# Four-layer graph network: one sign flipped in layer 0, one transpose of layer 3 moved to memory, the last graph's layer 3 in two halves

## The chip, the cores and the metric

One Trainium2 chip, one core of it. The metric is device time in microseconds (us): the median over the executions of one program. The engines are PE (matrix multiply; PEld is its weight load), DVE (vector), ACT (scalar, with the activation functions), POOL (GpSimd) and SP, which here only issues DMAs.

## The reference

64 graphs of 256 nodes with 128 features share one adjacency matrix `adj` (256 x 256). Four layers follow each other, each `x = x + layer(relu(layernorm(x)))`.

```
# layer 0, h = relu(layernorm(x)), e runs over 256 channels; W is adj
s1 = h @ W[:, :128].T ;  s2 = h @ W[:, 128:].T
pre[i,j,e] = s1[i,e] + s2[j,e] + b_lin[e]
e[i,j] = sum_e a[e] * leaky_relu(pre[i,j,e], 0.2) + adj[i,j]
out = sigmoid(softmax_j(e) @ h)
# layer 1: attention of one sigmoid per pair, masked by adj, two linear maps with elu
# layer 2: A = exp(8*tanh(q k'/sqrt(128)/8)) * adj, rows normalised;  out = A @ x @ v
# layer 3: five steps of a gated unit, av = [adj @ h, adj @ h]
z = sigmoid(av @ w3' + u3(h)); r = sigmoid(av @ w4' + u3(h))
hv = tanh(av @ w5' + (r*h) @ u5'); h = (1-z)*h + z*hv
```

Layer 0 is by far the most work: for each graph 256 x 256 x 256 values of `relu(s1 + s2 + b)`, each used once in a sum over channels. All is float32.

## The kernel before, in words

**Groups.** The graphs are taken in 34 groups: two of one graph, thirty of two graphs, two of one graph (`GROUPS`). Names below follow the profile: lines are those of the kernel before.

**Layer 0.** `head` (L558) makes, for a group, `s1` and its negative `s1n`, with channels on the partitions: two ACT instructions for each half of the channels, L576 and L578, both from the same PSUM tile. `senders` (L608) makes `s2` for one graph. The relu is written as a maximum: `relu(s1+s2) = max(s2, -s1) + s1`, and the `+ s1` is the same for all j and falls out of the softmax. So three engines make tiles of 128 channels x 256 senders, one per receiving node: ACT with `Relu(s2 + s1)` (L758), POOL with `max(min(s2, FLT_MAX), s1n)` (L763), DVE with `max(s2, s1n)` (L740), four or eight nodes in one instruction. PE multiplies the tiles by the weights `a` and sums over channels (`multiply`, L824). The weights stand in `a_win`, a column of +-0.8 in a field of zeros, of which a window of 32 columns is loaded so that node t falls in row t of the output. A batch is eight tiles (4 blocks of 32 rows x 2); where both tiles of a block have the same weight column, one matmul of 512 columns does them (four matmuls a batch), else two of 256 (eight a batch).

PE and the makers share work through merging: when enough batches wait for PE (`SPARE`), `begin` (L666) lays out the next two rows so that DVE adds the second channel half to the first (`merge`, L782) and PE gets three batches in place of four.

**Layers 1 to 3** run as chains of small pieces beside layer 0 of later graphs. Many transposes go through memory: `crossed` (L106) writes a tile to DRAM and reads it back with its two axes exchanged, both DMAs in SP's queue; the read is in pieces of 16 bytes for a group of two graphs. In layer 3 the groups 0 to 27 do so (`layer3_across`, L1206: state in after the norm, and after each of the first four steps); the state of the last step is transposed by PE into PSUM (`y_ps`, L151) and DVE adds it to x (L1269). Groups 28 to 33 (`layer3`) transpose by PE at every step (`hn_ps`). PSUM for layer 3 is one pool that the two lanes take in turn (the list `inside`).

**Order.** All engine instructions are written out by a planner (the loop from L1411 on). It keeps a clock for each engine, advanced by fixed costs per instruction, asks every chain when its next piece could start, and emits the piece or tile that starts first; at equal times the order of the list `chains` decides. A DMA read carries a planned landing time, and what uses it is not planned earlier. A change of cost anywhere therefore moves the order of tiles everywhere.

**The end.** When the last tile is made, layers 1 to 3 of the last graph (group 33) and layer 3 of groups 31 and 32 are left; they share PE. Group 33's layer 3 is 256 columns wide and uses the banks of `ps_e` and `ps_h` (`Home.LAST`).

Of the kernel before, what the change touches and what calls it, by code (L numbers as in the profile page):

```python
# [12 lines left out]
P = 128  # L13
# [61 lines left out]
def kernel(ctx: ExitStack, tc: tile.TileContext, ins: dict, out: bass.AP):  # L75
# [124 lines left out]
    a_win = constant([P, 2, 63], "a_win")  # L200
# [53 lines left out]
    blin_n = constant([P, 2], "blin_n")  # L254
# [3 lines left out]
    def constants0():  # L258
# [59 lines left out]
        dve(2).tensor_scalar(blin_n, b_ps, -1.0, None, ALU.mult)  # L318
        for half in (1, 0):
            yield "act"  # L320
            act(N).copy(w_p[:, half, :], p[:, half, :])
# [18 lines left out]
        for c in range(2):  # L340
            w = a_win[:, c, 31:32]
            dve(1).tensor_scalar(w, p_two[:, c : c + 1], n_pos, None, ALU.is_lt)
            dve(1).tensor_scalar(w, w, 1.6, -0.8, ALU.mult, ALU.add)

# [182 lines left out]
    def first_head(xt, to, snd):  # L527
# [14 lines left out]
        s1n = ap.tile([P, 2, W], F32, tag="s1n", name="s1n")  # L542
        for ec in range(2):
            dve(W, 1).tensor_scalar(
                s1n[:, ec, :], s1_ps[:, ec, :], -1.0, blin_n[:, ec : ec + 1], ALU.mult, ALU.add
            )
# [3 lines left out]
        s1 = ap.tile([P, 2, W], F32, tag="s1", name="s1")  # L550
        for ec in range(2):
            act(W, 1, more=27).activation(
                s1[:, ec, :], s1_ps[:, ec, :], AF.Identity, bias=blin_p[:, ec : ec + 1]
            )
        to.update(s1=s1, s1n=s1n)
        snd.update(s2=s2, s2_ps=s2_ps)

    def head(xt, to):  # L558
# [7 lines left out]
        for ec in range(2):  # L566
# [6 lines left out]
            if ec == 0:  # L573
                s1 = ap.tile([P, 2, W], F32, tag="s1", name="s1")
                s1n = ap.tile([P, 2, W], F32, tag="s1n", name="s1n")
            act(W, 1, more=27).activation(s1[:, ec, :], p, AF.Identity, bias=blin_p[:, ec : ec + 1])  # L576
            yield "act"
            act(W, 1, more=27).activation(  # L578
                s1n[:, ec, :], p, AF.Identity, bias=blin_n[:, ec : ec + 1], scale=-1.0
            )  # L580
        to.update(s1=s1, s1n=s1n)
# [53 lines left out]
    class Pairs:  # L635
# [5 lines left out]
        def __init__(self, g, b, of, snd):  # L641
# [9 lines left out]
            self.s1n_v = of["s1n"].rearrange("p c (g t k) -> p c g k t", g=4, k=G)[  # L651
# [14 lines left out]
        def begin(self):  # L666
# [7 lines left out]
            for t, ec, on_top, two in kinds:  # L674
                batch = {
                    "t": t, "ec": ec, "merged": on_top, "two": two, "halves": 0, "ready": 0.0
# [42 lines left out]
        def make(self, who):  # L719
# [9 lines left out]
            s1, s1n = self.of["s1"], self.of["s1n"]  # L729
            if who == "dve":  # L730
# [4 lines left out]
                if batch["two"]:  # L735
                    s1n = self.s1n_v[:, ec, 2 * g2 : 2 * g2 + n, 1, t : t + 2].unsqueeze(3)
                else:
                    s1n = self.s1n_v[:, ec, 2 * g2 : 2 * g2 + n, :, t : t + 1]
# [4 lines left out]
                    s1n.to_broadcast([P, n, 2, N]),  # L743
                    ALU.max,
# [7 lines left out]
            else:  # L752
                for g, ic, i in self.nodes(batch, g2):
                    if g > 2 * g2 or ic:
                        yield
                    if who == "act":
                        model.op("act", model.TILE["act"] + 42 * (s2 is self.snd["s2"]))
                        nc.scalar.activation(  # L758
                            r[:, g, ic, :], s2[:, ec, :], AF.Relu, bias=s1[:, ec, i : i + 1]
                        )  # L760
                    else:
                        model.op("pool", model.TILE["pool"])
                        nc.gpsimd.tensor_scalar(  # L763
                            r[:, g, ic, :], s2[:, ec, :], FLT_MAX, s1n[:, ec, i : i + 1],
# [7 lines left out]
        def merge(self):  # L772

            _, batch, g2 = self.merges.pop(0)
            r = batch["r"]
            for g, ic, i in self.nodes(batch, g2):
                if ic:
                    continue
                if g > 2 * g2:
# [3 lines left out]
                    r[:, g, ic, :], self.own("dve")[:, 1, :], self.of["s1n"][:, 1, i : i + 1],  # L783
                    r[:, g, ic, :], ALU.max, ALU.add,
# [18 lines left out]
        def multiply(self):  # L803
# [11 lines left out]
            elif batch["ec"]:  # L815
                parts = ((0, t, 0, 0), (1, t, 1, 1))
            else:
                parts = ((slice(0, 2), t, 0, slice(0, 2)),)
            for ic, t, sign, k in parts:
                for g in range(4):  # L820
                    to, of = self.e_ps[bass.ts(g, 32), ic, :], r[:, g, k, :]
                    if len(parts) == 1:
                        to, of = to.rearrange("p a b -> p (a b)"), flat(of)
                    nc.tensor.matmul(  # L824
                        to, lhsT=a_win[:, sign, 31 - t : 63 - t], rhs=of,
# [101 lines left out]
    def layer1(x1, h, h_t, at, last):  # L927
# [33 lines left out]
        yield "pool"  # L961
# [62 lines left out]
    def layer2(x2, by_memory):  # L1024
        G, NB, W = sizes(x2)
        h = yield from ln_relu(bp, x2, "h2", "h")
# [4 lines left out]
        else:  # L1031
            h_t = yield from by_pe(h, "h_t", when=free_a)
            yield "pe"
        g_ps = psum_a([P, W], "g_ps")
# [5 lines left out]
        hv_ps = psum_a([P, G, P], "hv_ps")  # L1040
# [7 lines left out]
        for b in range(NB):  # L1048
            yield "pe"
            s_ps = psum_a([P, 2, N], "s2_ps")  # L1050
# [477 lines left out]
```

## Time and profile before

| what | value |
|---|---|
| median of 3 runs | 4942.22 us (4939.57 to 4942.91) |
| the profiled execution's own time | 4945.24 us |
| its span | 4943.5 us |
| PE busy | 4882.2 us (99%) |
| DVE busy | 4855.4 us (98%) |
| ACT busy | 4824.6 us (98%) |
| POOL busy | 4773.1 us (97%) |
| DMA queue of SP, share of 16 engines | 73.8% |
| mean granted clock of PE | 1.0 |

Busy time of a group is the union of its instructions' intervals, and "mean ns of one" is the length of one from its start to its end. The engines overlap the end of one instruction with the start of the next, so what an instruction costs its engine is the distance from its start to the start of the one behind it, read from the timeline; it is shorter than the mean. A matmul in float32 shows as two records, so that four matmuls are eight.

### The profile page before, as it was taken

To read this page: it belongs to the slowest core of one execution; us is meant where nothing else is said; L and a number is where in the kernel's file an instruction comes from. 1 tells how busy PE (TensorE), PEld (TensorE's weight loads), DVE (VectorE), ACT (ScalarE), POOL (GpSimd) and SP (SyncE) were. 2 spreads that over 40 slices of the span, in tenths; PEclk is the share of its full clock that TensorE was granted. 3 is DMA by queue.
4 is the path that set the end of the run, shared out by engine and by line. 5 is a ranking of instruction groups with operands and counts; after the bars stand their busy time and mean duration, and the time that the engine had idled before them with its cause. 6 is when DMAs were issued, how large, how long until landed. Compare 5 with 4: busy or idle time off the path is not lost.

```text
span 4943.5 us, 176182 instructions
## 1 busy us (share of the span) xinstructions
PE 4882.2 (99%) x69407; PEld 2392.8 (48%) x69407; DVE 4855.4 (98%) x8488; ACT 4824.6 (98%) x12590; POOL 4773.1 (97%) x10419
## 2 busy tenths in 40 slices
PE   9999999999999999999999999999999999999998
PEld 4445544444554454545544544445444544445444
DVE  9999999999999999999999999999999999999994
ACT  8999999999999999999999999999999999999994
POOL 8999999999999999999999999999999999999891
PEclk9999999999999999999999999999999999999999
DMA  1559989989799889898898797787776777773220
GB/s 24 21 17 32 33 35 39 39 33 40 35 35 39 40 32 43 34 36 39 34 40 36 36 39 37 32 44 36 34 40 35 38 37 37 36 37 22 17 15 6
DMA packets 4456815, 165.39 MB, mean 33 GB/s; under 512 B 4386992, under 2 KB 4423728, under 8 KB 4455984
## 3 DMA queue, kind: packets, MB, share of 16 engines
q1 hardware_dynamic: 4455440, 153.86, 73.8%
q8 instruction: 544, 8.91, 1.0%
q14 instruction: 287, 2.35, 0.3%
q10 hardware_dynamic: 544, 0.26, 0.0%
HBM read 77.73 MB, written 76.35 MB: 31 GB/s over the span
## 4 chain that ended last, share of the span: by engine, by line
PE 50%; DVE 36%; ACT 5%; issue 2%; POOL 1%; DMA 0%; DVEq 0%; SPq 0%; ACTq 0%; POOLq 0%
PE e_ps L824 31%; DVE r L740 15%; DVE r L782 14%; PE gate_ps L144 4%; ACT r L758 3%; PE hv_ps L144 3%; PE m_ps L144 3%; PE s_ps L144 2%; PE o_ps L144 1%; PE e_ps L144 1%; PE rc_ps L144 1%; DVE bst L479 1%; PE rsum_ps L144 1%; DVE gate_ps L1255 1%; DVE rh L1253 1%
## 5 line engine op out<-in xcount | busy, mean ns | idle before, releaser
L763 POOL TENSOR_SCALAR r<-s,s1n 128x256 f32<-128x256 f32 x10168 | 4600.2, 478 | 40.5 <-PE e_ps L824 24.5
L758 ACT ACTIVATE r<-s_act,s 128x256 f32<-128x256 f32 x9736 | 4041.1, 758 | 5.4 <-PE e_ps L824 5.4
L824 PE MATMUL e_ps<-r,a_win 128*32 128x256 f32 (+1 forms) x40960 | 3293.8, 464 | 10.2 <-DVE r L740 7.9
L740 DVE TENSOR_TENSOR r<-s_ps,s1n 128x2048 f32<-128x2048 f32 (+1 forms) x1313 | 2341.5, 1818 | 0.3 <-PE e_ps L824 0.3
L824 PEld LDWEIGHTS e_ps<-r,a_win 128*32 128x32 f32 x40960 | 1404.0, 110 | 1609.1 <-issue 884.7
L782 DVE SCALAR_TENSOR_TENSOR r<-s_ps,s1n,r 128x256 f32<-128x256 f32 x4096 | 1687.0, 469 | 0.2
L501 ACT ACTIVATE h<-xt,bsh,brs 128x128 f32<-128x128 f32 x512 | 302.1, 791 | 19.7 <-DVE bsh L491 19.2
L758 ACT ACTIVATE r<-s,s 128x256 f32<-128x256 f32 x512 | 271.6, 775 | 0.0
L144 PE MATMUL m_ps<-adj_q,hn 128*32 128x256 f32 x4096 | 248.3, 379 | 2.1 <-ACT hn L1193 2.1
L144 PEld LDWEIGHTS m_ps<-adj_q,hn 128*32 128x32 f32 x4096 | 162.1, 132 | 93.9 <-issue 32.8
L488 POOL TENSOR_TENSOR brs<-bve,neg_half 128x4 f32<-128x4 f32 (+1 forms) x136 | 134.0, 985 | 66.0 <-DVE bve L484 60.8
L144 PE MATMUL gate_ps<-m_t,w_t 128*32 128x512 f32 (+1 forms) x1360 | 170.0, 567 | 1.5 <-ACT m_ps L1153 1.4
L144 PE MATMUL gate_ps<-m_t,t_w_w 128*32 128x512 f32 (+1 forms) x1360 | 170.5, 568 | 0.3 <-ACT m_t L1143 0.2
L144 PE MATMUL hv_ps<-m_t,t_w_w 128*32 128x512 f32 (+1 forms) x1360 | 170.1, 567 | 0.0
L144 PE MATMUL hv_ps<-rh,u_th 128*32 128x512 f32 (+1 forms) x1360 | 169.7, 567 | 0.0
L144 PE MATMUL s_ps<-h_t,w_p 128*32 128x256 f32 (+1 forms) x1568 | 138.7, 452 | 3.8 <-DVE adj_l L618 3.2
L144 PE MATMUL gate_ps<-hf,u_t 128*32 128x512 f32 (+1 forms) x1088 | 136.9, 567 | 0.0
L1232 ACT COPY m_t<-m_ps 128x512 f32<-128x512 f32 (+1 forms) x140 | 130.8, 934 | 1.2 <-PE m_ps L144 1.2
L1250 ACT ACTIVATE hv_ps<-hv_ps,bh 128x512 f32<-128x512 f32 (+1 forms) x140 | 128.7, 919 | 0.0
L1248 ACT ACTIVATE gate_ps<-gate_ps,bz 128x512 f32<-128x512 f32 (+1 forms) x140 | 127.5, 911 | 0.0
L1236 ACT ACTIVATE m_ps<-gate_ps,br 128x512 f32<-128x512 f32 (+1 forms) x140 | 116.4, 831 | 7.1 <-PE gate_ps L144 6.8
L479 DVE BATCH_NORM_STATS2 bst<-xt 128x6 f32<-128x128 f32 x512 | 120.6, 276 | 1.9 <-DMA xt<-in_x_dram 1.6
(220 smaller groups left out, 3847.4 us busy)
## 6 DMA issues: line engine op xcount, KB each, us to landing
there<-hf SPq DMA_DIRECT2D x104, 256.0 KB
hn<-there SPq DMA_DIRECT2D x104, 256.0 KB
there<-h SPq DMA_DIRECT2D x86, 256.0 KB
there<-pm SPq DMA_DIRECT2D x62, 256.0 KB
pt<-there SPq DMA_DIRECT2D x62, 256.0 KB
h_t<-there SPq DMA_DIRECT2D x60, 256.0 KB
xt<-in_x_dram SPq DMA_DIRECT2D x30, 256.0 KB
out_dram<-xt SPq DMA_DIRECT2D x30, 256.0 KB
```

What stands on the lines that cost most here:

```text
L144: nc.tensor.matmul(out[bass.ts(c, 32)], lhsT=lhsT[:, bass.ts(c, 32)], rhs=rhs, **flags)
L479: dve(P).bn_stats(st[:, g, :], xt[:, g, :])
L488: pool(1085).tensor_tensor(rstd, ve, neg_half[:, 0:G], ALU.pow)
L501: act(P, 2, 1).activation(h[:, 0:P, g], xt[:, g, :], AF.Relu, bias=shift[:, g : g + 1], scale=rstd[:, g : g + 1],)
L740: nc.vector.tensor_tensor(r[:, 2 * g2 : 2 * g2 + n, :, :], s2[:, ec : ec + 1, :].unsqueeze(1).to_broadcast([P, n, 2, N]), s1n.to_broadcast ...
L758: nc.scalar.activation(r[:, g, ic, :], s2[:, ec, :], AF.Relu, bias=s1[:, ec, i : i + 1])
L763: nc.gpsimd.tensor_scalar(r[:, g, ic, :], s2[:, ec, :], FLT_MAX, s1n[:, ec, i : i + 1], ALU.min, ALU.max,)
L782: nc.vector.scalar_tensor_tensor(r[:, g, ic, :], self.own("dve")[:, 1, :], self.of["s1n"][:, 1, i : i + 1], r[:, g, ic, :], ALU.max, ALU.add,)
L824: nc.tensor.matmul(to, lhsT=a_win[:, sign, 31 - t : 63 - t], rhs=of, start=False, stop=self.over, skip_group_check=True,)
L1232: act(W).copy(m_t, m_ps)
L1248: act(W, 1).activation(g_ps, g_ps, AF.Tanh, bias=bz, scale=0.5)
L1250: act(W, 1).activation(hv_ps, hv_ps, AF.Tanh, bias=bh)
```

## The change

- The half of the combined weights that makes `s2` is negated once (`w_p`), so `s2` holds `-s2`. DVE and POOL now take a minimum with `s1` itself, which is minus the value before; ACT's relu takes `scale=-1.0` and keeps its sign. `s1n` and `blin_n` are gone, and with them L578 of every group.
- The sign of a tile now depends on who made it, so `a_win` has two sets of weights, and each half batch notes in `up` whether ACT made it. A merged batch of which ACT made a part has two signs side by side (the merged tile is always negative, its neighbour positive); it goes to PE as eight matmuls of 256 columns, not four of 512. A merge subtracts where ACT made the first part.
- In `layer3_across` the last state too goes through memory (`crossed(..., "y3")`), and DVE adds the tile that comes back; the PE transposes `y_ps` of groups 0 to 27 are gone.
- Group 33's layer 3 is two chains, one for each half of its nodes (128 columns), with PSUM banks of their own; each step's transposed state is needed by both halves. Its last sum has another form: `0.5*(z+1)*cand - 0.5*(z-1)*h`, with `0.5*h` made by ACT ahead of time. Layer 2 of group 33 uses the free banks of `ps_e`. Group 32's banks are others, and `chains` is ordered anew.

```diff
-    a_win = constant([P, 2, 63], "a_win")
+    a_win = constant([P, 2, 2, 63], "a_win")
...
-            act(N).copy(w_p[:, half, :], p[:, half, :])
+            act(N).activation(
+                w_p[:, half, :], p[:, half, :], AF.Copy, scale=-1.0 if half else 1.0
+            )
...
-            w = a_win[:, c, 31:32]
+            w, w_n = (a_win[:, up, c, 31:32] for up in (1, 0))
...
+            dve(1).tensor_scalar(w_n, w, -1.0, None, ALU.mult)
...
# head
-            yield "act"
-            act(W, 1, more=27).activation(
-                s1n[:, ec, :], p, AF.Identity, bias=blin_n[:, ec : ec + 1], scale=-1.0
-            )
...
# Pairs.make
-                    s1n.to_broadcast([P, n, 2, N]),
-                    ALU.max,
+                    s1.to_broadcast([P, n, 2, N]),
+                    ALU.min,
...
+                batch["up"][g2] = int(who == "act")
...
-                            r[:, g, ic, :], s2[:, ec, :], AF.Relu, bias=s1[:, ec, i : i + 1]
+                            r[:, g, ic, :], s2[:, ec, :], AF.Relu, bias=s1[:, ec, i : i + 1],
+                            scale=-1.0,
...
-                            r[:, g, ic, :], s2[:, ec, :], FLT_MAX, s1n[:, ec, i : i + 1],
+                            r[:, g, ic, :], s2[:, ec, :], s1[:, ec, i : i + 1], -FLT_MAX,
                             ALU.min, ALU.max,
...
# Pairs.merge
-                    r[:, g, ic, :], self.own("dve")[:, 1, :], self.of["s1n"][:, 1, i : i + 1],
-                    r[:, g, ic, :], ALU.max, ALU.add,
+                    r[:, g, ic, :], self.own("dve")[:, 1, :], self.of["s1"][:, 1, i : i + 1],
+                    r[:, g, ic, :], ALU.min, ALU.subtract if up else ALU.add,
...
# Pairs.multiply
+            elif batch["merged"] and any(batch["up"]):
+                parts = ((0, t, 0, 0), (1, t, 0, 1))
...
+                    up = 0 if batch["merged"] and k == 0 else batch["up"][g // 2]
...
-                        to, lhsT=a_win[:, sign, 31 - t : 63 - t], rhs=of,
+                        to, lhsT=a_win[:, up, sign, 31 - t : 63 - t], rhs=of,
...
# layer2: bank = last_bank if last else psum_a, and the same in its six uses of psum_a
...
-        LAST = ((ps_e, "e"), (ps_e, "e"), (ps_h, "ps_h"))
-        LAST_BUT_ONE = ((ps_h, "ps_h"), (ps_c, "s2_act"))
+        LAST_BUT_ONE = ((ps_a, "ps_a"), (ps_c, "s2_act"))
...
+    def layer3_half(x3, c, of):
+        H = P
+        space, tag = ((ps_e, "e"), (ps_h, "ps_h"))[c]
...
+        for step in range(STEPS):
+            m_t, t_r, rh2, half, keep, cand, new, node = (t[:, c] for t in of.work[step % 2])
+            whole_new, whole_node = of.work[step % 2][6:8]
+            yield "pe", None, of.nodes[step][1 - c]
+            hf = of.hf[c]
+            m_ps = bank("m_ps")
+            for mc in range(2):
+                mm(
+                    m_ps, lhsT=of.hn[mc], rhs=adj_q[:, mc, bass.ts(c, H // 2), :],
+                    start=(mc == 0), stop=(mc == 1),
+                )
+            g_ps = bank("gate_ps")
+            mm(g_ps, lhsT=u3_t, rhs=hf, start=True, stop=False)
+            yield "act"
+            act(H).copy(m_t, m_ps)
+            yield "pe"
+            mm(g_ps, lhsT=ws["w4_w"], rhs=m_t, start=False, stop=True)
+            hv_ps = bank("hv3_ps")
+            mm(hv_ps, lhsT=ws["w5_w"], rhs=m_t, start=True, stop=False)
+            yield "act"
+            act(H, 1).activation(t_r, g_ps, AF.Tanh, bias=br, scale=0.5)
+            act(H, sbuf=1).activation(half, hf, AF.Copy, scale=0.5)
+            yield "dve"
+            dve(H).scalar_tensor_tensor(rh2, t_r, 1.0, hf, ALU.add, ALU.mult)
+            yield "pe"
+            mm(g_ps, lhsT=w34_t, rhs=m_t, start=False, stop=True, skip_group_check=True)
+            mm(hv_ps, lhsT=u5_th, rhs=rh2, start=False, stop=True)
+            yield "act"
+            act(H, 1).activation(g_ps, g_ps, AF.Tanh, bias=bz, scale=0.5)
+            act(H, 1).activation(cand, hv_ps, AF.Tanh, bias=bh)
+            yield "dve"
+            dve(H).scalar_tensor_tensor(keep, g_ps, 1.0, half, ALU.subtract, ALU.mult)
+            dve(H, more=60).scalar_tensor_tensor(g_ps, g_ps, 1.0, cand, ALU.add, ALU.mult)
+            dve(H, more=120).scalar_tensor_tensor(new, g_ps, 0.5, keep, ALU.mult, ALU.subtract)
+            of.hf[c] = new
+            of.state[step][c][0] = model.t["dve"] + LAG["dve"]
+            yield "pe", None, of.state[step][1 - c]
+            tp = bank("hn_ps")
+            mm(
+                tp, lhsT=pairs(whole_new.rearrange("p c n -> p (c n)"))[:, :, c], rhs=ident,
+                start=True, stop=True,
+            )
+            if step < STEPS - 1:
+                yield "act"
+                act(H).copy(node, tp)
...
+        yield "dve"
+        dve(H).tensor_tensor(x3[:, c, :], tp, x3[:, c, :], ALU.add)
+        nc.sync.dma_start(out=of_group(out, len(GROUPS) - 1)[:, c, :], in_=x3[:, c, :])
...
# layer3_across
-            if step < STEPS - 1:
-                hn, at = crossed(h, "hn" + tag, "hn", "dve")
-        yield "pe", lambda: not inside
-        inside.append(lane)
-        tp = psum([P, G, P], "y_ps")
-        turn()
-        for g in range(G):
-            tr(tp[:, g, :], h[:, :, g])
-        yield "dve"
-        dve(W).tensor_tensor(x3, tp, x3, ALU.add)
-        inside.remove(lane)
+            hn, at = crossed(h, "hn" + tag, "hn" if step < STEPS - 1 else "y3", "dve")
+        yield "dve", None, at
+        dve(W).tensor_tensor(x3, hn.rearrange("p f g -> p g f"), x3, ALU.add)
...
-    chains = [ahead, behind, chain5, *lanes, chain2, chain1, chain4]
+    chains = [ahead, behind, chain5, chain6, chain4, *lanes, chain2, chain1]
```

## The prediction

> **What bounds the kernel now.** I read the page first, then the busy time by stretches, the waits of each engine, the timeline of each engine in the middle, and the chain of waits at the end.
>
> The page:
>
> ```profile
> span 4943.5 us, 176182 instructions
> PE 4882.2 (99%) x69407; PEld 2392.8 (48%) x69407; DVE 4855.4 (98%) x8488; ACT 4824.6 (98%) x12590; POOL 4773.1 (97%) x10419
> ...
> L763 POOL TENSOR_SCALAR r<-s,s1n 128x256 f32<-128x256 f32 x10168 | 4600.2, 478 | 40.5 <-PE e_ps L824 24.5
> L758 ACT ACTIVATE r<-s_act,s 128x256 f32<-128x256 f32 x9736 | 4041.1, 758 | 5.4 <-PE e_ps L824 5.4
> ```
>
> Four engines are full at once, so no single one can be relieved with profit: the planner hands tiles from one maker to another, and by merging from PE to DVE. The time falls only by what the work of all four falls. One stretch from the middle of the busy time by stretches (length; busy time of PE, PEld, DVE, ACT, POOL; clock; DMA share; GB/s):
>
> ```profile
> 1854.00:1977.60 123.60, 123.36 (x1748) 58.96 (x1744) 123.43 (x214) 123.30 (x325) 121.17 (x264) 1.00 1.01 43
> ```
>
> DMA's 16 engines show full here as well, yet the waits of DVE, ACT, POOL and PE hold a single one on a DMA, 1.6 us long, for the first load:
>
> ```profile
> DVE bst L479 <- DMA xt<-in_x_dram: 1.6, 1, 1.6
> ```
>
> So DMA is late for nobody. The end is another regime: the last tile's matmul is over at 4836, and 107 us follow in which PE serves three chains of layer 3 and in the last 13 us only one. The chain of waits there:
>
> ```profile
> 4936.70 0.91 PE hv_ps L144 x16
> 4937.63 0.46 ACT hv_ps L1173
> 4938.11 0.44 DVE df L1177
> 4938.57 0.44 DVE gate_ps L1180
> 4939.04 0.43 DVE hf L1183
> 4939.61 0.49 PE y_ps L151 x2
> ```
>
> One engine works at a time: group 33's last step runs from its transpose at 4932.30 to that at 4939.61, 7.31 us.
>
> **The change part by part.** Counts are those of the built order of instructions, before and after. Costs are distances from start to start in the timeline of the middle:
>
> ```profile
> 2103.06 0.85 ACT L576 ACTIVATE s<-s_ps,blin_p 128x512 f32<-128x512 f32 x1
> 2103.63 1.37 ACT L758 ACTIVATE r<-s_act,s 128x256 f32<-128x256 f32 x3
> 2104.70 0.88 ACT L578 ACTIVATE s1n<-s_ps,blin_n 128x512 f32<-128x512 f32 x1
> 2105.27 2.13 ACT L758 ACTIVATE r<-s_act,s 128x256 f32<-128x256 f32 x5
> 2107.05 0.82 ACT L1232 COPY m_t<-m_ps 128x512 f32<-128x512 f32 x1
> ```
>
> *ACT.* L578 costs 2105.27 - 2104.70 = 0.57 us, like L576 (2103.63 - 2103.06). That pair also answers what `scale=-1.0` costs a tile: L578 has it, L576 not, and they are equal, so nothing. Gone are 60 of them and 6 of 256 columns (0.36 us, as a tile: 2107.05 - 2105.27 = 1.78 for five): 34.2 + 2.2 = 36.4 us. The planner fills that with 68 more tiles (9736 to 9804), 68 x 0.357 = 24.3. Net -12.1.
>
> ```profile
> 2122.16 1.04 PE L824 MATMUL e_ps<-r,a_win 128*32 128x256 f32 x16
> 2123.02 1.04 PE L144 MATMUL g_ps<-h_t,qk 128*32 128x512 f32 x8
> 2123.99 0.75 PE L151 MATMUL y_ps<-ident,hf 128*128 128x128 f32 x4
> 2124.67 1.92 PE L824 MATMUL e_ps<-r,a_win 128*32 128x512 f32 x16
> ...
> 4861.29 1.04 PE L144 MATMUL gate_ps<-hf,u_t 128*32 128x512 f32 x8
> 4862.15 1.05 PE L144 MATMUL rc_ps<-e_t,y 128*32 128x256 f32 x16
> ```
>
> *PE.* A group's last transpose costs 2124.67 - 2123.99 = 0.68 us. 26 groups of two graphs and two of one (0.45 each) lose it: -18.6. Against that, tiles of ACT in merged batches break the wide form: 8192 matmuls of 512 become 5352, 12288 of 256 become 18008, that is 2048 and 1536 batches become 1338 and 2251. Five batches more in all, 5 x 0.86 = +4.3. The other 710 change form. A narrow batch, 16 records, takes 2123.02 - 2122.16 = 0.86; a wide one, 8 records, 4862.15 - 4861.29 = 0.86; 16 narrow records of `m_ps` elsewhere take 0.865. I take 5 ns a batch, +3.6. Net -10.7.
>
> Here a rule speaks against the change. The Trainium skill, "TensorE: Matmul & The Clock Gate", section "LDWEIGHTS (loading the stationary operand)", gives a weight load P/1.2 ns for P columns, about 27 ns for these 32. 5,760 more records of loads (2 x (5720 - 2840)), none hidden, would by that page be an estimated +155 us of PE and a loss. The equal 0.86 says that all are hidden, and the sum goes by it.
>
> *DVE.* Merges fall from 4096 to 4056; one costs 0.392 (eight from 2043.21 to 2046.35): -15.7. Full tiles 751 to 744 at 2.20 (two from 2054.20 to 2058.60), half tiles 562 to 576 at 1.13 (2059.20 to 2060.33): +0.4. `min` for `max` and `subtract` for `add` keep shape and operands: nothing. The sum into x (L1269) reads two SBUF tiles where it read one and PSUM; no row has that at 512 columns. The nearest, L1258, has one of each and takes 0.60; 0.1 more or less would be 3 us in all, and I take 0. Net -15.3.
>
> *POOL.* 28 tiles fewer (10168 to 10140) at 0.452 (86 of them in 38.85): -12.7. The pointer moves from second to first scalar; the trace has no such POOL row. Nearest is DVE's TENSOR_SCALAR with the pointer first (L898, mean 736 ns for 512 columns), against 674 for a sum without one, so a pointer is worth 0.06 us there. The tile before has one too, only elsewhere, so I take no difference; 0.06 either way would be 600 us of POOL, and the upper side is a rival.
>
> *DMA.* 26 + 2 crossings more on SP's queue, each a store and a read. 73.8% of 16 engines over 4943.5 us is 13.1 ns for each of 4455440 packets; a read of 128 x 128 pieces is 16384, so 13.4 us of all sixteen, and 27 full ones 362 us: about 81%. What waits for it is the sum into x, on DVE, and behind that DVE's tiles. SP's queue is in order: the store waits for the state (its likes waited for `hf` L1258 76 times, 1014.7 us, 27.8 at most), and behind it stand the other lane's and layer 0's transfers. It is off every path as long as all of these land by their planned times; they do so now with the same waits in the queue. A lane's next group starts one crossing later, some 20 us of the 300 between two groups of a lane. Cost 0; if each were 1 us late, 28.
>
> A rule against this part too: the Trainium skill, "DMA: Bandwidth & Descriptors", section "Specifications", wants at least 512 bytes a piece for line rate, and these reads are in 16. The trace agrees that they are slow (33 GB/s mean at 74% busy), and shows that nobody waits.
>
> *Together, in steady state:* PE -10.7, ACT -12.1, POOL -12.7, DVE -15.3. The fullest engine there is DVE (123.43 of 123.60), PE has the least relief. I take -12, between -8 (PE alone decides and loses a little more order) and -16.
>
> *The start.* DVE makes the first `s1` alone while ACT copies `s2`; two ACT pieces of 0.4 go from the way to the first tile, two tiny DVE pieces and a memset twice as long come. -0.5, between -1 and 0.
>
> *The end.* Group 33's layer 3 takes 4884.56 to 4940.1, 55.5 us. Its matmuls and those of the two others in that time, each at its distance, sum to 43 us before, and to 42 in the order after: PE was idle or waiting for 23%. Halving a step's width shortens each link: PE's by 1.5 us (six matmuls of 0.43 on the path become five of half that, the sixth goes ahead), ACT's four by some 0.12 each (L1173 takes 448 ns at 256 columns, 753 at 512), DVE's four by 0.13 (L1183: 424 and 680). 7.3 becomes about 5, plus some 0.5 for the other half in front. Three groups now end together, so nobody runs alone for 13 us. With a wait share of 15%, 42/0.85 = 50 us: -5. Bounds: -10 when PE runs dense, +2 when twice as many small instructions queue on ACT and DVE.
>
> *Sum:* -12 - 5 - 0.5 = -17.5. On the profiled execution's 4945.24 that is 4927.7; it lies 3.0 above the median of the runs, so 4924.7, and I say 4925. The bounds alone give 4915 to 4936.
>
> **The rivals.** Two tenths of a per cent, 9.9 us, is about what a measurement of this kernel can tell from no change.
>
> *No gain worth the name* (0.14): the steady part does not come through, because the narrow batches cost more in long rows than in the stretches shown. 710 at 15 ns more eat PE's 10.7; the end's 5 stays: 4937. For it: PE has the smallest relief. Against: 0.86 in both forms.
>
> *Slower, by the form of POOL's tile* (0.07): the pointer as first scalar takes longer. Each nanosecond is 10 us of POOL; spread over four makers by a plan that does not know it, at least a quarter of that, at most all. From 2 to 7 ns more the gain is gone; 10 ns make about +8 to +80, say 4965. Against: shape, count of operands and operations are the same.
>
> *Slower, by late landings* (0.05): 27 x 1.5 us of DVE standing still is +40, so 4965; it decides from 0.65 us each. For: the stretch with DMA share 1.01. Against: no wait on any of 250 reads so far.
>
> *Forecast* (0.74): 4915 to 4936. Range to hold 8 of 10: a little into the no-gain case above, the largest bounds below: 4910 to 4940. Faster by over 0.2% takes the forecast; slower the last two.
>
> **What would show it.** Right: L578 and the `y_ps` of L1269 gone; the narrow batch still 0.86 us; POOL's tile 0.452; no wait on `y`; the last `e_ps` some 12 us earlier, and about 102 us from there to the end. Wrong: POOL's or ACT's mean up by ten nanoseconds, DVE waiting for DMA, PE idle for weight loads, or an end as long as before.

## The result and the profile after

| | before | after |
|---|---|---|
| median of 20 runs each | 4943.24 us (4939.57 to 4946.58) | 4951.27 us (4944.08 to 4956.63) |
| ratio | | 1.0016, 95% interval [1.001, 1.0022] |
| profiled execution, its span | 4945.24, 4943.5 us | 4952.73, 4950.9 us |

The change made the kernel slower by 8 us. The forecast was 4925, with 4940 as its upper end.

The page of after, its span, its engines and the groups that make tiles:

```profile
span 4950.9 us, 188006 instructions
PE 4876.8 (99%) x75409; PEld 2685.0 (54%) x75409; DVE 4856.2 (98%) x8477; ACT 4817.8 (97%) x12624; POOL 4750.5 (96%) x10391
...
L757 POOL TENSOR_SCALAR r<-s,s 128x256 f32<-128x256 f32 x10140 | 4577.4, 478 | 44.5 <-PE e_ps L821 29.5
L751 ACT ACTIVATE r<-s_act,s 128x256 f32<-128x256 f32 x9804 | 4043.1, 780 | 5.4 <-PE e_ps L821 5.1
```

What was foretold of tiles is there: 28 POOL tiles fewer at the same mean of 478 ns, 68 ACT tiles more, the second piece of ACT per half of `s1` gone. Still every engine finishes later, and POOL is idle for longer in a longer span. So the time went to something that none of these rows shows.

The operations on `y`, the tile that the last state comes back in, are the place. This is the view of one tile; the columns are count, shortest/median/longest in ns, first and last start. The first line is after's sum into x, the second before's (there the tile is `y_ps`, in PSUM):

```profile
L1322 DVE TENSOR_TENSOR xt<-y,xt x28: 408/1164/3290, 559.2 to 4548.9; 128x512 f32<-128x512 f32 x26, 128x256 f32<-128x256 f32 x2
```

```profile
L1269 DVE TENSOR_TENSOR xt<-y_ps,xt x28: 404/672/682, 539.7 to 4534.3; 128x512 f32<-128x512 f32 x26, 128x256 f32<-128x256 f32 x2
```

Same operation, same shape, but the median is 1.7 times as long and the longest nearly five times. From start to start the 28 sums cost DVE 35.8 us, where they cost 16.2: +19.6. And POOL pays for the same moments. Here is one ordinary sum, DVE's timeline and then POOL's:

```profile
822.85 1.25 DVE L776 SCALAR_TENSOR_TENSOR r<-s_ps,s,r 128x256 f32<-128x256 f32 x3
824.02 1.17 DVE L1322 TENSOR_TENSOR xt<-y,xt 128x512 f32<-128x512 f32 x1
825.09 0.49 DVE L776 SCALAR_TENSOR_TENSOR r<-s_ps,s,r 128x256 f32<-128x256 f32 x1
```

```profile
823.95 1.51 POOL L757 TENSOR_SCALAR r<-s,s 128x256 f32<-128x256 f32 x1
```

The tile takes 1.51 us instead of 0.48: it stands still while the sum runs. Of POOL's 10140 tiles 29 are longer than 650 ns, and 28 of them lie beside a sum, one beside each; these 28 are 23.0 us over 480 ns each. In the trace of before 2 of 10168 are longer, worth 0.6 us together, and none lies beside a sum.

It also goes the other way. The place where PE loses most, first DVE, then POOL and then PE:

```profile
1996.14 3.19 DVE L1322 TENSOR_TENSOR xt<-y,xt 128x512 f32<-128x512 f32 x1
1999.26 0.47 DVE L776 SCALAR_TENSOR_TENSOR r<-s_ps,s,r 128x256 f32<-128x256 f32 x1
```

```profile
1992.91 7.99 POOL L757 TENSOR_SCALAR r<-s,s 128x256 f32<-128x256 f32 x16
```

```profile
1992.70 3.84 PE L821 MATMUL e_ps<-r,a_win 128*32 128x256 f32 x44
2000.78 0.66 PE L144 MATMUL left_ps<-h_t,left 128*32 128x256 f32 x8 [4.24 <-DVE r L776]
```

Here POOL's tiles run on while the sum waits (the records give four of 0.47 us begun after it, then one of 1.27). The sum takes 3.19 us, DVE's tiles behind it are late, and PE stands still for 4.24 us. (The longest sum, 3.29 us at 4265.77, looks the same, and PE then waits 3.38 us.) The planner counts the same for this sum as for the one before. PE's waits for DVE's tiles in front of `left_ps` stand in two rows. The one for DVE's L776, as here, rose from 3.5 us in before to 5.1. The other in after, and behind it the same row in before (there the line is L740; total us, times, longest):

```profile
PE left_ps L144 <- DVE r L732: 18.8, 15, 3.4
```

```profile
PE left_ps L144 <- DVE r L740: 6.2, 7, 1.2
```

Summed over the trace from 150 to 4560 us, PE's idle time rose from 28.7 to 43.0 us, ACT's from 26.7 to 46.3, POOL's from 21.1 to 47.8.

The loss does not come from the end: from the last `e_ps` matmul to the last record there are 101.1 us against 107.0, but that matmul is over at 4849.9 instead of 4836.4. Counted by the end of layer 0 of each of the 64 graphs (DVE's sum of `adj_j` into `e_ps`), after was up to 17 us ahead at graph 25 and lost it all after that.

### The profile page after: what moved, and what is told of

It is laid out like the page before. It is cut to its first block, busy times and chain, and to the rows that moved or that the text cites. A ratio compares the mean times of both kernels' runs of the same rounds, so it can differ in the third digit from the quotient of the medians.

```text
span 4950.9 us, 188006 instructions
## 1 busy us (share of the span) xinstructions
PE 4876.8 (99%) x75409; PEld 2685.0 (54%) x75409; DVE 4856.2 (98%) x8477; ACT 4817.8 (97%) x12624; POOL 4750.5 (96%) x10391
## 3 DMA queue, kind: packets, MB, share of 16 engines
q1 hardware_dynamic: 4918688, 168.02, 81.1%
## 4 chain that ended last, share of the span: by engine, by line
DVE 50%; PE 41%; ACT 3%; issue 3%; POOL 3%; DMA 0%; DVEq 0%; SPq 0%; POOLq 0%; ACTq 0%
PE e_ps L821 25%; DVE r L732 21%; DVE r L776 18%; PE gate_ps L144 4%; ACT r L751 3%; PE m_ps L144 3%; PE hv_ps L144 2%; POOL r L757 2%; PE s_ps L144 1%; PE o_ps L144 1%; DVE bst L480 1%; DVE gate_ps L1315 1%; PE e_ps L144 1%; DVE rh L1313 1%; DVE hf L1318 1%
## 5 line engine op out<-in xcount | busy, mean ns | idle before, releaser
L757 POOL TENSOR_SCALAR r<-s,s 128x256 f32<-128x256 f32 x10140 | 4577.4, 478 | 44.5 <-PE e_ps L821 29.5
L821 PE MATMUL e_ps<-r,a_win 128*32 128x256 f32 (+1 forms) x46720 | 3331.6, 428 | 9.7 <-DVE r L732 9.5
L821 PEld LDWEIGHTS e_ps<-r,a_win 128*32 128x32 f32 x46720 | 1678.7, 110 | 1440.9 <-issue 629.5
L732 DVE TENSOR_TENSOR r<-s_ps,s 128x2048 f32<-128x2048 f32 (+1 forms) x1320 | 2343.2, 1809 | 1.4 <-PE e_ps L821 1.4
L776 DVE SCALAR_TENSOR_TENSOR r<-s_ps,s,r 128x256 f32<-128x256 f32 x4056 | 1671.3, 469 | 0.3 <-ACT r L751 0.3
L751 ACT ACTIVATE r<-s,s 128x256 f32<-128x256 f32 x512 | 283.9, 867 | 0.9 <-DVE s L545 0.9
L144 PEld LDWEIGHTS m_ps<-adj_q,hn 128*32 128x32 f32 x4032 | 164.1, 132 | 78.0 <-issue 21.1
```

What stands on the lines that cost most here:

```text
L144: nc.tensor.matmul(out[bass.ts(c, 32)], lhsT=lhsT[:, bass.ts(c, 32)], rhs=rhs, **flags)
L732: nc.vector.tensor_tensor(r[:, 2 * g2 : 2 * g2 + n, :, :], s2[:, ec : ec + 1, :].unsqueeze(1).to_broadcast([P, n, 2, N]), s1.to_broadcast( ...
L751: nc.scalar.activation(r[:, g, ic, :], s2[:, ec, :], AF.Relu, bias=s1[:, ec, i : i + 1], scale=-1.0,)
L757: nc.gpsimd.tensor_scalar(r[:, g, ic, :], s2[:, ec, :], s1[:, ec, i : i + 1], -FLT_MAX, ALU.min, ALU.max,)
L776: nc.vector.scalar_tensor_tensor(r[:, g, ic, :], self.own("dve")[:, 1, :], self.of["s1"][:, 1, i : i + 1], r[:, g, ic, :], ALU.min, ALU.su ...
L821: nc.tensor.matmul(to, lhsT=a_win[:, up, sign, 31 - t : 63 - t], rhs=of, start=False, stop=self.over, skip_group_check=True,)
```

## The experiments

The theory, T: DVE's sum of two tiles in SBUF and POOL's tiles shut each other out. Rivals: the sign change and its narrow batches cost more than thought (R1); only the read of `y` in steps of 16 bytes is slow (R2); 28 more transfers through memory land late or disturb (R3). The level of the kernel before differed between chips (4943 us on some, 4956 on others), so a time is compared only with those of the same chip.

### The last state by PE again

In the changed kernel the last state goes back through PE, as before; sign change and halves stay.

```
-            hn, at = crossed(h, "hn" + tag, "hn" if step < STEPS - 1 else "y3", "dve")
-        yield "dve", None, at
-        dve(W).tensor_tensor(x3, hn.rearrange("p f g -> p g f"), x3, ALU.add)
+            if step < STEPS - 1:
+                hn, at = crossed(h, "hn" + tag, "hn", "dve")
+        yield "pe", lambda: not inside
+        ...
+        for g in range(G):
+            tr(tp[:, g, :], h[:, :, g])
+        yield "dve"
+        dve(W).tensor_tensor(x3, tp, x3, ALU.add)
```

> The changed kernel with the last state of layer 3 transposed by PE again, as before; sign and halves stay. Theory (the sum x + y of two SBUF tiles on DVE and POOL's tiles hold each other up): with the sum on a PSUM tile again, DVE's sum is back at 0.67 us long and POOL's tile beside it at 0.48; by the counts of the built order PE has 5 us less than before, DVE 5, ACT 9, POOL 11, so the last e_ps comes 5 to 10 us earlier than before and the end is 6 us shorter: 4928 to 4934. Rival (the loss comes from the sign: narrow batches and tiles of mixed sign stretch layer 0): still 4945 or more. It does not tell the sum from the 28 crossings themselves.

Measured: 4939.73 us, ratio 0.9967 [0.9955, 0.998] where before took 4956.57. The last `e_ps` is over at 4836.3, as early as in the first profile of before and not 5 to 10 us earlier, so the time lies between the theory's range and the rival's. On a second chip with before at 4955.76:

> The whole change but with the last state sent back through PE, on a chip whose kernel before may run at 4943 instead of 4957. Theory (the sum of two SBUF tiles on DVE and POOL's tiles shut each other out): the sum is 0.68 us again, the last e_ps at about 4836 or earlier, ratio to before 0.9965 to 0.9995, that is 4926 to 4941 where before is 4943. If instead the sign change or the narrow batches cost the time, 1.000 to 1.002.

Measured: 4940.78, ratio 0.9969 [0.9958, 0.9981]. And on a third with before at 4942.9, beside the changed kernel itself and another profile of before:

> The whole change but with the last state sent back through PE, beside the changed kernel itself. Theory: 4939 to 4942 us whatever the kernel before does, 10 to 12 us under the changed kernel; ratio to before 0.9993 where before is 4943 and 0.9968 where it is 4956.

> The changed kernel beside the kernel before once more. Theory (the sum of two SBUF tiles costs the changed kernel its gain, whatever the kernel before does): 4951 us, 10 to 12 us above the version without that sum run beside it; ratio to before 1.0016 where before is 4943 and 0.999 where it is 4956. If the changed kernel shared the level of the kernel before, it would be at 4964 where before is 4956.

> The kernel before, profiled once more, for its level: 4943 or 4956 us. If the level is one of the work between 150 and 4560 us, PE's idle time there is up from 28.7 us by some 10; if it is one of the end, the time from the last e_ps to the end is up from 107 us.

Measured: 4937.25, ratio 0.999 [0.9981, 0.9999], and the changed kernel beside it 4950.87, 1.0018 [1.0009, 1.0027]. So this one edit is worth 13.6 us, a little more than the 10 to 12 expected, and without it the change wins. The profile of before there was that of a 4941.22 us run, alike the first one (PE's idle time 26.0 us, 107.0 from the last `e_ps`). In the trace of the version by PE the sum is as short as ever, and one POOL tile of 10144 is longer than 650 ns:

```profile
L1329 DVE TENSOR_TENSOR xt<-y_ps,xt x28: 416/684/699, 540.7 to 4555.5; 128x512 f32<-128x512 f32 x26, 128x256 f32<-128x256 f32 x2
```

PE's wait for DVE's tiles is back to where it was:

```profile
PE left_ps L144 <- DVE r L732: 7.9, 8, 1.6
```

R1 falls as the cause of the loss: sign change and narrow batches are in this kernel. R3 still stands, and so does T.

### The memory crossing alone

The kernel before, with nothing but the last state through memory.

```
-            if step < STEPS - 1:
-                hn, at = crossed(h, "hn" + tag, "hn", "dve")
-        yield "pe", lambda: not inside
-        ...
+            hn, at = crossed(h, "hn" + tag, "hn" if step < STEPS - 1 else "y3", "dve")
+        yield "dve", None, at
+        dve(W).tensor_tensor(x3, hn.rearrange("p f g -> p g f"), x3, ALU.add)
```

> The kernel before with only the last state of layer 3 through memory and the sum on DVE from two SBUF tiles. Theory: the sum takes 1.1 to 3.3 us on DVE where it took 0.67, and the POOL tile beside it 1.2 to 1.5 where it took 0.48, 20 us on each; PE loses 18.6 us of transposes. Slower than before by 5 to 20 us, 4948 to 4963, with PE waiting for DVE tiles behind the late sums. Rival (the loss is the sign's): PE's relief comes through, 4933 to 4943.

Measured: 4983.86, ratio 1.0054 [1.004, 1.0068]. The loss comes with this part alone, but it is larger than the theory's 5 to 20 us. That it is 27 us here and 13.6 in the comparison above is not explained: in its trace the 28 sums cost DVE 34.1 us, no more than in after, and PE's idle time is 49.0 us.

```profile
L1262 DVE TENSOR_TENSOR xt<-y,xt x28: 426/1158/2582, 557.8 to 4603.2; 128x512 f32<-128x512 f32 x26, 128x256 f32<-128x256 f32 x2
```

### Memory, but no sum of two SBUF tiles

The crossing stays in the changed kernel; ACT copies `y` to PSUM and DVE sums from there.

```
-        yield "dve", None, at
-        dve(W).tensor_tensor(x3, hn.rearrange("p f g -> p g f"), x3, ALU.add)
+        yield "act", lambda: not inside, at
+        inside.append(lane)
+        tp = psum([P, G, P], "y_ps")
+        act(W, sbuf=1).copy(tp, hn.rearrange("p f g -> p g f"))
+        yield "dve"
+        dve(W).tensor_tensor(x3, tp, x3, ALU.add)
+        inside.remove(lane)
```

> The changed kernel, the tile from memory copied by ACT into a PSUM bank of layer 3 and summed by DVE from there. All crossings stay. Theory: DVE's sum is 0.67 us long, POOL's tile beside it 0.48, and for 0.52 us of ACT a group the rest of the change comes through: 4925 to 4935. Rival (28 more crossings are late or in the way): 4945 to 4955 as the changed kernel.

Measured: 4940.77, ratio 0.9967 [0.9955, 0.998], as good as by PE on that chip (4939.73), though between the two ranges expected.

```profile
L1324 ACT COPY y_ps<-y x28: 1269/1726/2477, 558.9 to 4554.7; 128x512 f32<-128x512 f32 x26, 128x256 f32<-128x256 f32 x2
...
L1326 DVE TENSOR_TENSOR xt<-y_ps,xt x28: 410/681/706, 561.3 to 4557.2; 128x512 f32<-128x512 f32 x26, 128x256 f32<-128x256 f32 x2
```

All 28 transfers are still there, and the loss is gone although ACT pays 28.8 us for the copies: R3 falls. One POOL tile is longer than 650 ns. ACT's copy is not seen to wait through anything (the longest costs 1.38 us), but is slow as well, 1.065 us from start to start where another ACT copy of 512 columns takes 0.47 to 0.52. So the 16-byte step has a price of its own.

### Without the step

DVE sums the two tiles in the order they lie in memory, so x receives a permuted state. Everything else is the changed kernel.

```
-        dve(W).tensor_tensor(x3, hn.rearrange("p f g -> p g f"), x3, ALU.add)
+        dve(W).tensor_tensor(flat(x3), flat(hn), flat(x3), ALU.add)
```

> The changed kernel whose sum reads y in the order in which it lies in SBUF, without the step of 16 bytes; so features and nodes are mixed up in the sum for groups 0 to 27, and x there is not the reference's. Theory (two SBUF tiles against POOL): nothing changes, the sum stays at 1.1 us or more with cases of 2 to 3, POOL's tile beside it 1.2 to 1.5, total 4947 to 4955. Rival (the step in the read makes it slow): the sum falls to 0.6 to 0.7, POOL's tile is 0.48, total about 4930 to 4936.

Measured: 4944.7, ratio 0.9977 [0.9968, 0.9986], 5 us above the version by PE on the same chip and again between the two ranges.

```profile
L1322 DVE TENSOR_TENSOR xt<-y,xt x28: 408/801/3253, 559.5 to 4541.3; 128x512 f32<-128x512 f32 x26, 128x256 f32<-128x256 f32 x2
```

Without the step the 28 sums cost DVE 23.1 us, 6.9 over before, and POOL's tiles over 650 ns make 13.9 us more than 480 each; with it +19.6 and 23.4. One sum still takes 3.25 us, with five POOL tiles begun after it before it gets its turn. So T and R2 both hold: the lock is there without the step, and the step makes it longer, because the sum itself is slower (the shortest of 512 columns costs 1.01 us from start to start with the step and 0.60 without).

### The sum on POOL, and the planner told

Two kernels ask how the sum costs time. In one, POOL makes the sum:

```
-        yield "dve", None, at
-        dve(W).tensor_tensor(x3, hn.rearrange("p f g -> p g f"), x3, ALU.add)
+        yield "pool", None, at
+        pool(1265).tensor_tensor(x3, hn.rearrange("p f g -> p g f"), x3, ALU.add)
```

> The whole change, but the sum of y into x on POOL instead of DVE. Theory: DVE is not shut out any more and no POOL tile is made beside it, so the stalls of 2 to 3 us go, PE's idle time between 150 and 4560 us falls from 43 to about 30 us. POOL pays for the sum itself: 28 times 1.3 us if the 16-byte step costs POOL nothing, 2 to 2.5 us if it halves its rate as on DVE and ACT; DVE is relieved of 28 times 1.08. Time between before and after: 4939 to 4947 where before is 4943. If late landings were the cause, POOL would wait instead, 20 us or more, and the time would stay at 4951.

In the other, the planner counts the lost time when it places the sum, and the instructions stay as they are:

```
         yield "dve", None, at
-        dve(W).tensor_tensor(x3, hn.rearrange("p f g -> p g f"), x3, ALU.add)
+        model.op("pool", 850 * G // 4)
+        dve(W, more=480 * G // 4).tensor_tensor(x3, hn.rearrange("p f g -> p g f"), x3, ALU.add)
```

> The changed kernel as it is on the chip, but the planner counts 480 ns more of DVE and 850 ns more of POOL at each of the 28 sums. If the loss is mostly the surprise (the planned order breaks, PE waits for late tiles), most of it goes: 4943 to 4947, PE's idle time falls towards 30 us. If it is mostly the work lost on DVE and POOL (28 x 1.3 us shared by four engines, 9 us), little goes: 4948 to 4952, with some tiles moved to ACT. In both cases the sums stay at 1.1 us and longer.

Measured, on one chip with the second run by PE (4940.78): sum on POOL 4946.9, ratio 0.9983 [0.9975, 0.9992]; planner told 4953.24, 0.9996 [0.9987, 1.0004].

On POOL the sum never waits long, and the step costs it something, against POOL's other sum of 512 columns without one (first the view of the tile, then the other sum's group; its mean of 1224 ns has four sums of 256 columns in it, the median of all 34 is 1286):

```profile
L1322 POOL TENSOR_TENSOR xt<-y,xt x28: 772/1592/1684, 559.1 to 4552.5; 128x512 f32<-128x512 f32 x26, 128x256 f32<-128x256 f32 x2
```

```profile
L960 POOL TENSOR_TENSOR xt<-xt,bm_bc 128x512 f32<-128x512 f32 (+1 forms) x34 | 41.6, 1224 | 1.2 <-ACT h L502 1.2
```

POOL loses 42 us to the sums, PE's idle time is 36.0 us where about 30 was expected, and the time still lies 6 us below the kernel whose planner was told. That kernel has fewer stalls, as one of the two expectations had it (PE idle 32.7 us, from 43.0), and is 12.5 us above the version by PE all the same; it missed both ranges. What the planner could avoid as a stall came back as work: PE's idle time fell by 10.3 us, and its busy time rose by 9.1, to 4885.9 from 4876.8. Counting the lost time in the plan does not remove the loss.

### The other two parts by themselves

The sign change alone, on the kernel before (`w_p` negated, no `s1n`, minima, a second sign in `a_win`):

```
-            act(W, 1, more=27).activation(
-                s1n[:, ec, :], p, AF.Identity, bias=blin_n[:, ec : ec + 1], scale=-1.0
-            )
...
-                    ALU.max,
+                    ALU.min,
...
-                        to, lhsT=a_win[:, sign, 31 - t : 63 - t], rhs=of,
+                        to, lhsT=a_win[:, up, sign, 31 - t : 63 - t], rhs=of,
```

> The kernel before with the sign alone: no s1n, minima, two sets of weights, narrow batches. Theory: all makers have 5 to 11 us less to do (built order: PE -5, DVE -5, ACT -9, POOL -11), nothing else changes, the end stays: 5 to 11 us faster than before. Rival (narrow batches and mixed signs stretch layer 0): no gain or slower.

Measured: 4939.86, ratio 0.9995 [0.9986, 1.0004]; before there 4942.58. The 5 to 11 us of the theory are not there, and what there is cannot be told from nothing. Once more, where before took 4955.76:

> The sign change alone (s2 negated, no -s1 tile, minima), on the chip of the run above. Theory: it gives 3 to 8 us, ratio 0.9984 to 0.9995; the last state by PE as before, so the sum stays at 0.68 us. If narrow batches eat the gain: 1.000. The difference to the run above is what the two halves of the last graph's layer 3 are worth once the sum is out of the way: between -3 and +3 us.

Measured: 4942.39, ratio 0.9976 [0.9967, 0.9985]; this ratio goes with the higher level of before, and the time itself is no lower than on the other chip. With the halves of the last graph beside it (the run by PE) it is 4940.78 there, so the halves are worth 1.6 us at that place, which these runs cannot tell from nothing. The halves alone, on the kernel before:

```
-        LAST = ((ps_e, "e"), (ps_e, "e"), (ps_h, "ps_h"))
...
+            of = Halves(hn, h_t)
+            for c, chain in enumerate((chain5, chain6)):
+                chain.add(layer3_half(xt, c, of))
+            return
```

> The kernel before with the last group's layer 3 in halves, its layer 2 on free banks and the new order of chains. The counts of tiles are those of before. Theory: layer 0 ends when it did, the end is 5 to 6 us shorter, and the whole by as much: ratio 0.9988 to 0.9990. Rival (the order of chains moves layer 0 too): anything beyond 5 us either way, visible in the time of the last e_ps.

Measured: 4944.2, ratio 1.0004 [0.9995, 1.0013]. The 5 to 6 us expected are not there. The end is 109.8 us from the last `e_ps` instead of 107: group 33's layer 3, counted from its first `m_ps`, takes 57.4 us to the end where it took 58.9, but starts 52.4 us after the last `e_ps` where it started 48.1.

The changed kernel and the kernel before, unaltered, in the same rounds as these two:

> The changed kernel itself beside the parts of it, on the same chip. If the sum on DVE is what costs it (theory), it is slower than the kernel without that part by the 15 to 25 us that separate the two in the first runs; ratio to before 1.000 to 1.003.

> The kernel before, for a trace from the chip of the parts. The runs of before here were 13 us above those of the prediction's chip. If that chip is slower in one kind of work, the trace shows which; if the kernel's order only meets a few long waits, the tiles cost what they did and the idle time is larger.

Measured: 4951.4, ratio 1.0017 [1.0008, 1.0026], and 4942.34 for the profiled run of before. The changed kernel is 11.5 us above the sign change alone on that chip, less than the 15 to 25 expected.

### One chip on which the loss is larger

> The kernel before, profiled once more. On a chip where it takes 4956 us: if the 13 us lie in the work between 150 and 4560 us, PE's idle time there is up from 28.7 us by some 10; if in the end, the 107 us from the last e_ps to the end are up. On a chip where it takes 4943 us: as in the first profile.

> The changed kernel beside the kernel before. Theory: 4950 to 4953 us on any chip, so the ratio to before is 1.0016 where before takes 4943 and 0.999 where it takes 4956. If the changed kernel shares the level of the kernel before: 4964 where before takes 4956, ratio 1.0016 again.

Measured: the changed kernel 5002.42, ratio 1.0057 [1.0043, 1.007]; before 4976.65 in the rounds, but 4943.56 in its own profiled run on that chip. 5002 lies beyond both expected times, and the ratio is a third kind of answer: the loss itself is larger here, some 26 us. The trace of the changed kernel there tells what became larger: the page's group of POOL's tiles, the sums, and the longest of them on DVE with POOL beside it.

```profile
L757 POOL TENSOR_SCALAR r<-s,s 128x256 f32<-128x256 f32 x10140 | 4604.2, 549 | 47.7 <-PE e_ps L821 22.4
```

```profile
L1322 DVE TENSOR_TENSOR xt<-y,xt x28: 415/1466/9121, 560.9 to 4598.0; 128x512 f32<-128x512 f32 x26, 128x256 f32<-128x256 f32 x2
```

```profile
4483.16 9.12 DVE L1322 TENSOR_TENSOR xt<-y,xt 128x512 f32<-128x512 f32 x1
```

```profile
4481.76 9.68 POOL L757 TENSOR_SCALAR r<-s,s 128x256 f32<-128x256 f32 x21
```

POOL's tiles start as often as elsewhere (0.449 us apart, median) but last 549 ns on average instead of 478, so that a tile overlaps the next by 0.10 us instead of 0.03. Ten of the 28 sums cost over 2 us (three in the first trace of after), one lies beside nineteen tiles, and all 28 come to 69.4 us of DVE. This fits a sum that can begin only when it falls between two tiles; that POOL's longer tiles cause it was not tested by itself. PE's idle time there is 68.6 us.

What stays open is the level of the kernel before, which hardly has such sums: 4943, 4956 and 4977 us on different chips. No profile of it at one of the higher levels exists, since its profiled run was at 4943.56 on the slowest chip too. The level is not fixed by the chip alone: where before took 4955.76, one of its 28 runs took 4945.26 and the others 4952 to 4961. The traces of its relatives differ in one thing that may bear on it. POOL's tiles, where one follows another, start 448.4 ns apart on average in some versions with the sign change and 450.8 in others, both on one chip (the second run by PE, and the second of the sign change alone); in the memory crossing alone it is 454.1, in before 451.8. Some 2.4 ns on each of 10,000 tiles are 24 us of POOL. Whether this makes the level was not tested.

## Why the prediction was wrong

**The step that failed** is the term in the paragraph on DVE: "The sum into x (L1269) reads two SBUF tiles where it read one and PSUM; no row has that at 512 columns. The nearest, L1258, has one of each and takes 0.60; 0.1 more or less would be 3 us in all, and I take 0." Measured: 0.70 us more each on DVE (19.6 in 28), and 0.8 each on POOL (23.0 in 28), which the term did not count at all. It was wrong in its size, and in the belief that a sum on DVE costs DVE alone.

And a row did exist. In the first 40 us of the trace of before DVE combines two SBUF tiles of 512 columns once (L416), and one POOL tile runs beside it:

```profile
37.40 0.73 DVE L416 SCALAR_TENSOR_TENSOR mask_h<-adj_q,mask_h 128x512 f32<-128x512 f32 x1
```

```profile
37.57 0.90 POOL L763 TENSOR_SCALAR r<-s,s1n 128x256 f32<-128x256 f32 x1
```

That tile takes 0.90 where its neighbours take 0.47. It is one of only two of 10168 over 650 ns, and would have priced the lock without the step at 0.4 us a sum on POOL, some 12 us for 28.

The Trainium skill had the rule, "SBUF — State Buffer", section "Who interferes with whom": "A DVE instruction with two SBUF inputs contends with a GpSimd instruction that reads SBUF". Its section "SBUF: two separate sides" says that the one that starts first keeps the shared ports for its whole instruction and the other stands still. The runs agree for the ordinary case that one stands still (1.51 us of a POOL tile beside a sum of 1.17). Which one started first the records do not tell: that tile begins 0.07 us before the sum and stands still all the same. A sum that waits while four and more tiles begun after it run is more than the page states.

**Steady state, "I take -12".** Most signs of being right came true, and still the last `e_ps` came 13.4 us later, not 12 earlier. The sign change's terms came out as rows: ACT's second piece is gone, `scale=-1.0` costs nothing (a tile is 0.356 us from start to start in both traces), POOL's pointer in the other place does not slow its tile (448.4 ns from start to start on average, against 451.8), and a narrow batch takes what a wide one does:

```profile
2104.32 1.04 PE L821 MATMUL e_ps<-r,a_win 128*32 128x512 f32 x8
2105.18 1.04 PE L144 MATMUL s_ps<-h_t,w_p 128*32 128x512 f32 x8
2106.03 1.04 PE L821 MATMUL e_ps<-r,a_win 128*32 128x256 f32 x16
2106.90 1.04 PE L144 MATMUL gate_ps<-m_t,w_t 128*32 128x512 f32 x8
```

0.86 and 0.87. So the rivals of the narrow batches and of POOL's form named the wrong causes. ACT's mean length did rise, from 758 to 780 ns, which the prediction had named as a sign of being wrong; but the length is not the cost, since a tile takes 838 ns in the third run by PE, which is faster than before. The 27 ns that the prediction gives a load of 32 columns are not those of this case: in the trace of before it lasts 110 ns on average, and is hidden even so.

How the loss came about can be reckoned, after the fact, from two profiles of the third chip, the changed kernel and the version by PE (idle time from 150 to 4560 us). The changed kernel has 17.2 us more work on DVE in the sums (33.4 against 16.2), 23.0 more on POOL beside them and the 18.6 of transposes less on PE: a mean over the four engines of +5.4. The idle times of PE, DVE, ACT and POOL differ by +11.8, +2.0, +16.1 and -6.2, a mean of +5.9. Together +11.3, where the last `e_ps` came 9.4 later. So about half of the loss is work, and half is waiting, which the forecast held constant.

**A second step failed, apart from the sums:** "The time falls only by what the work of all four falls", taken as a gain that comes through. For the version by PE the counts gave PE -5, DVE -5, ACT -9 and POOL -11, a mean of -7.5; its last `e_ps` came only 0.1, 2.0 and 1.5 us earlier, on three chips, than in the first profile of before. In the third of these profiles POOL's busy time up to the last `e_ps` is 43.0 us lower than in that of before and DVE's 10.2, but POOL is idle for 41.5 us more and DVE for 8.7, and the busy times of PE and ACT are within 1 us of before's. The relief of two engines was not handed on to the other two. For POOL part of it is the shorter tile, which the planner's fixed cost (454 ns in both kernels) does not know: POOL's idle time from 150 to 4560 us is 28.2 us in the first run by PE, where the tiles start 450.8 ns apart, and 49.3 in the third, where it is 448.4. Why the rest was not handed on stays open.

**PE's relief.** The transposes (18.6 us) are gone, but at 19.6 us on DVE and 23.0 on POOL.

**DMA.** The share was forecast at 81% and is 81.1% on the page. Nobody waits for `y`; the sum's kernel through PSUM shows the crossings to be harmless. The rival of late landings had the right place (DVE at the sum), and even a fitting price: "it decides from 0.65 us each". Its mechanism was wrong, since the wait is for POOL.

**The end, "-5".** From the last `e_ps` 101.1 us against 107.0 looks like a hit, and is one only in part. The last tile itself is made at 4844.0 in after and at 4834.2 in before, so that from the last tile to the end there are 106.9 against 109.3 us, and the halves alone gave no gain in the runs. The size was off: group 33's layer 3, forecast 5 us shorter, takes 56.7 us from its first `m_ps` to the end, 2.2 less than before.

**The start** (-0.5) is not told apart by any run.

## What to carry to other kernels

Before an operand is moved from PSUM to SBUF, look at what the other input of that DVE instruction is, and at what POOL does meanwhile: in these runs two SBUF inputs on DVE beside a busy POOL cost both engines. That the price grows with how densely POOL is packed is suggested by one trace and was not tested. A rare instruction at the start of the trace, in no large group, can be the row that prices a new operation; look for the tiles that are longer than their fellows and at what runs beside them. And count an engine's relief as a gain only where the plan can use it: here most of POOL's became idle time. The version with the sign change and the halves but the last state by PE beats both kernels: 4937.25 us, 0.999 [0.9981, 0.9999] of before, where the changed kernel is at 1.0018.

## What was new of the hardware

A sum on DVE with two SBUF inputs does not always get its turn after one POOL tile: it waited through four (3.19 us) or five (3.25 us) begun after it and, where POOL's tiles overlap more, lay beside nineteen (9.12 us). What decides between a short and a long wait was not found. Reading float32 from SBUF in steps of 16 bytes slows DVE (a median of 1.08 us a sum of 512 columns against 0.75 without the step, both beside POOL; the shortest 1.01 against 0.60), takes about twice the time on ACT (1.065 against at most 0.52), and costs POOL's sum some 0.3 us on top of 1.29. In the groups of one graph, where the step is 8 bytes, the shortest sums are as fast as from PSUM (408 and 404 ns for 256 columns).
